# GpSimd makes h, TensorE takes its maximum over partitions, and integers are made further ahead

## The chip, the cores and the metric

The kernel runs on one core of one Trainium2 chip. A core has five engines that work beside each other, each through its own queue in order: TensorE (PE; its weight loads are shown apart as PEld), VectorE (DVE), ScalarE (ACT), GpSimd (POOL) and SyncE (SP), which issues most of the transfers between the chip's memory and the core's. The metric is the time of one execution on the device, in microseconds (us). Beside the times there is one profiled execution, with a record of every instruction; its times are counted from the start of its span.

## The reference

Two layers are computed on x, 2 x 2048 rows of 512 columns. First comes a cross attention to a context of 2 x 128 rows, then a feed-forward block whose values are rounded to integers at each step:

```
def act_qdq(x):                       # 16 bits, one scale for the whole tensor
    scale = max(max(abs(x)) / 32767, 1e-12)
    return clip(round(x / scale), -32768, 32767) * scale
x = x + softmax(layernorm(x) @ Wq @ key.T / sqrt(512)) @ value     # key, value = ctx @ Wkv
h = act_qdq(layernorm(x))                                          # (4096, 512)
up   = act_qdq(h @ lpbq_dequant(w_up).T)                           # (4096, 1536)
gate = act_qdq(h @ lpbq_dequant(w_gate).T)
gate = act_qdq(gate * fixed_qdq_u16(sigmoid(gate)))                # called p below
o    = act_qdq(gate * up)
x = x + o @ lpbq_dequant(w_down).T
```

`lpbq_dequant` rounds the weights to 4 bits with a scale for each block of 32. What shapes the kernel is that each `act_qdq` needs the largest absolute value of a whole tensor before the first of its values can be rounded.

## The kernel before, in words

The 4096 rows are worked on in 8 groups of 512 (NG = 8, TG = 512), each as 4 tiles of 128 rows (NJ = 4). The 512 columns are 4 chunks of 128 (ND = 4), the 1536 columns of the feed-forward block 12 chunks (NF), taken in three tiles of four (NK = 3, NQ = 4). Products of integers with weights are exact: an integer is split into parts (a high part `a` = n/4096, a low part n - 4096a, and a third), and so is a weight; the first two parts go into a sum q, the third into a sum e, and the result is q times a constant less e. One projected chunk is 8 matmuls for q and 4 for e (L528 and L532), each of 512 columns.

The code is a straight list of instructions. A scheduler gives each engine its order: an earlier line goes first if it is ready by the scheduler's own estimate. `in_order(a, b, ...)` (L158) fixes that b is issued behind a on their engine. Tiles come from pools, and a pool's tile waits until the tile that had its place has been read for the last time.

*Attention* (L257 to L506), in the order of a loop over i from 0 to 8 (L477). In step i the kernel loads x of group i + 2 (`load_x`, into a place of four `far` tiles, so it waits for the last reader of group i - 2), transposes the softmax of group i - 1 (`turn`, eT: four transposes on TensorE and a copy out of PSUM by ScalarE, L419), makes the scores of group i (`scores`), adds the attention of group i - 1 to x (`attend`: a matmul po, and on VectorE L432, which leaves the row's sum), starts group i + 1 (`front`: transposes, bn_stats), turns h of group i - 2 (`lift`: 16 transposes, two copies into hT by ScalarE, L472), and makes h of group i - 1 (`normalise`). `normalise` is a chain of small steps: the negative mean (VectorE, L446), four squares with a sum (ScalarE, L449), variance (L456), its inverse root as a power on GpSimd (L284), the product with the mean (L458), and four times h = x * rstd + nmean (ScalarE, L460). VectorE then takes the largest absolute value of h into hmax (L503). In step 8 the last group goes through this tile by tile (L490 to L494). Between these, `advance(gate_steps, n)` splits the gate's weights, a block in some ten steps, most of them on VectorE (L179 to L201).

*Gate* (L534 to L588). `over_partitions` (L136) reduces hmax to one value a partition (L140) and takes the maximum over partitions on GpSimd (L142). `act_scale` makes s_h and its inverse r_h (L151, L153). Four instructions on VectorE round group 0 chunk by chunk into hi[0] (L542), and `split_integers` (L229) makes its parts: for each chunk a (VectorE, L235), the cast to part 0 (ScalarE, L236), part 1 and part 2 (VectorE, L237, L238). Behind that, one activation loads the table of the sigmoid (L546), and the integers of groups 1 to 7 are made in one go, odd groups by VectorE (L549), even ones by ScalarE (L551). Then hT's place is given up, and two g4 tiles, a second home for parts and the place in which up's and down's weights are split take it. For each group and tile, four chunks are projected, evacuated by ScalarE (L579), lessened by e on VectorE with a running maximum (L580), and stored. After each chunk, `advance(steps, 1)` goes on with the weights.

*Up* (L597 to L791) goes through the 24 tiles from the last group to the first (`order`), each in two halves c = 2j and 2j + 1. For a half, TensorE makes two chunks, ScalarE evacuates them (L726), VectorE subtracts (L727), SP stores. `next_gelu` makes the rounded gate and its sigmoid for the next tile by three passes of ScalarE (L624 to L626) into one of three buffers; it is called in the first half of every tile and once more at c = 1 and c = 13. `integers_of_p` (L658) makes p from them on VectorE (L661) and stores it, at the head of each tile. `bound` (L667) takes the largest product of |up| and p in each half, which later tells from which half tile the largest o comes: `fetch_best` (L674) finds the row by partition and gathers it with two indirect transfers on GpSimd's queue (L685), of which the first waits for the stores of up. `load_down` (L694) loads down's weights into the places of up's weights that are done with. At the end, the largest |up| goes over partitions through TensorE (L764 to L769): m_u is transposed as 128 equal columns, and VectorE reduces the rows.

*Down* (L794 to L1024). From the three candidate maxima comes `top` on GpSimd (L791), from it a_o, and `scale_of_o` (L907) makes six small values: k_o, with which p * up is rounded, and s_o, q_o and e_o, with which sums are scaled on their way out. A flag tells whether the shortcut holds; its value is read by every engine for a branch (L926), which isn't taken here. Then 32 blocks of 128 rows are rounded (`round_o`), split and multiplied (L874, L882).

Of the kernel before, what the change touches and what calls it, by code (L numbers as in the profile page):

```python
# [49 lines left out]
F32 = mybir.dt.float32  # L50
# [13 lines left out]
P = 128  # L64
# [12 lines left out]
def tile_xattn_ffn(  # L77
# [58 lines left out]
    def over_partitions(*stats, name):  # L136
# [6 lines left out]
        return [a[:, i : i + 1] for i in range(len(stats))]  # L143

# [112 lines left out]
    with ExitStack() as c0:  # L257

        with ExitStack() as c1:
# [153 lines left out]
            def turn(g, e):  # L413
# [5 lines left out]
                nc.scalar.copy(eT, pe)  # L419
# [22 lines left out]
            def normalise(g, js, h, total, nmean, squares, ve, rstd):  # L442
# [16 lines left out]
                for j in js:  # L459
                    nc.scalar.activation(  # L460
                        h[:, j, :], xt[:, j, :], AF.Identity, bias=nmean[:, j : j + 1], scale=rstd[:, j : j + 1]
                    )
# [43 lines left out]
            lift(NG - 1, hs.pop(NG - 1))  # L506

# [15 lines left out]
        def project(w, parts, q, e):  # L523


            for c in range(ND):
                for s in range(2):
                    nc.tensor.matmul(  # L528
                        q, lhsT=w[:, s, c, :], rhs=parts[:, s, c, :], start=(c + s == 0), stop=(c + s == ND)
                    )  # L530
            for c in range(ND):
                nc.tensor.matmul(e, lhsT=w[:, 2, c, :], rhs=parts[:, 2, c, :], start=(c == 0), stop=(c == ND - 1))  # L532

        with ExitStack() as c2:  # L534
            wg = [load_parts(wg_d, f, "wg") for f in range(NF)]
            s_h, r_h = act_scale(*over_partitions(hmax, name="h"), "h")
# [4 lines left out]
            for c in range(ND):  # L541
                nc.vector.tensor_scalar(hi[0][:, c], hT[:, c, :TG], r_h, QMAX, ALU.mult, ALU.min)  # L542
            first = split_integers(wk1, homes[0], hi[0], [ND, TG], "g0", ND)

            table = const.tile([P, 1], F32, name="table")
            nc.scalar.activation(table, unit, AF.Sigmoid)  # L546
            for t in range(1, NG):
                if t % 2:
                    nc.vector.tensor_scalar(hi[t], hT[:, :, ts(t, TG)], r_h, QMAX, ALU.mult, ALU.min)  # L549
                else:  # L550
                    nc.scalar.activation(hi[t], hT[:, :, ts(t, TG)], AF.Copy, scale=r_h)  # L551
            hpool.__exit__(None, None, None)
            home1 = tc.tile_pool(name="parts1", bufs=1, side="right")
            homes.append(ctx.enter_context(home1))
            wk2 = c2.enter_context(tc.tile_pool(name="wkb2", bufs=2))
            wpp = c2.enter_context(tc.tile_pool(name="wprep", bufs=1))
# [3 lines left out]
            steps = chain(split_rows(wpp, ps_t, w_up, wu_d, "u"), split_down(wpp, ps_t))  # L560
            groups, wu = {}, []
            for t in range(NG):
# [8 lines left out]
                for k in range(NK):  # L571
                    n = t * NK + k
                    g4 = wk2.tile([P, NQ, TG], F32, tag="g4", name=f"g4_{n}")
# [474 lines left out]
```

## Time and profile before

| | us |
|---|---|
| runs shown: median of 3, lowest, highest | 1007.1, 1004.01, 1007.13 |
| the profiled execution: its own time | 1005.54 |
| its span | 1003.7 |
| attention, up to the last copy into hT | 0 to 173.0 |
| gate and up on TensorE | 177.0 to 720.0 |
| down, from the first matmul of o | 734.5 to 1000.7 |

The busy shares of the span are: PE 94%, PEld 76%, DVE 81%, ACT 55%, POOL 9%. A line of the page or of a table of stretches gives for each engine its busy time and the number of instructions; the last three numbers of a stretch are the granted TensorE clock (1.00 is full speed), the share of the DMA engines' time, and GB/s. A line of the timeline gives start, length, engine, line of the code, operation, output <- inputs, shape, count, and in square brackets how long the engine was idle before and what released it. Matmuls are pipelined, so a matmul's length is longer than its share: 24 of 512 columns at full clock take 5.44 us, 0.227 each.

### The profile page before, as it was taken

The numbers are of one execution on the slowest core, as the hardware profiler recorded it, in microseconds if no ns is written. First come the engines' busy times: TensorE is split into PE (matmuls) and PEld (weight loads), VectorE is DVE, ScalarE is ACT, GpSimd is POOL, SyncE is SP. The second block draws the span as 40 slices with busy tenths as digits, with TensorE's granted clock in tenths as the row PEclk, the third lists the DMA queues.
The fourth block names the chain that finished last, engine by engine and source line by source line (L and its number), as shares of the span: only waits on it lengthen the run. The fifth ranks groups of instructions, "written<-read, shape, count | busy, mean of one in ns | idle before, by whom it ended". The sixth has DMA issues, their size and how long they took to land. (4 is left out here: it accounts for less than half of the span.)

```text
span 1003.7 us, 11683 instructions
## 1 busy us (share of the span) xinstructions
PE 942.7 (94%) x4321; PEld 762.9 (76%) x4321; DVE 810.7 (81%) x1000; ACT 548.3 (55%) x652; POOL 89.6 (9%) x67
## 2 busy tenths in 40 slices
PE   6997884999999999999999999999779999999998
PEld 5765652788888878887788788888557888888886
DVE  4579874999998989645899789887889999888882
ACT  2277786532333223226998998897454445444331
POOL 0101111000000000000000000000011232222221
PEclk9999896999999999999999999999879999999999
DMA  9177652987886666698899798988885676755611
GB/s 345 32 304 283 220 220 79 401 313 303 330 355 248 265 210 210 224 353 328 306 363 375 258 366 328 378 320 328 288 311 215 206 269 222 250 190 160 245 66 43
DMA packets 103596, 263.72 MB, mean 263 GB/s; under 512 B 6064, under 2 KB 46000, under 8 KB 94832
## 3 DMA queue, kind: packets, MB, share of 16 engines
q1 hardware_dynamic: 102496, 259.02, 69.4%
q0 software_dynamic: 512, 2.88, 0.8%
q10 hardware_dynamic: 528, 1.05, 0.3%
q8 instruction: 34, 0.56, 0.2%
q14 instruction: 26, 0.21, 0.1%
HBM read 136.05 MB, written 126.88 MB: 262 GB/s over the span
## 5 line engine op out<-in xcount | busy, mean ns | idle before, releaser
L528 PE MATMUL q_g<-parts_g,wg 128*128 128x512 f32 x768 | 195.0, 394 | 5.1 <-ACT parts_g L236 5.1
L528 PEld LDWEIGHTS q_g<-parts_g,wg 128*128 128x128 f32 x768 | 143.5, 189 | 35.4 <-ACT parts_g L236 5.8
L579 ACT ACTIVATE g<-q_g 128x512 f32<-128x512 f32 x96 | 57.3, 599 | 169.6 <-PE q_g L528 158.9
L528 PE MATMUL q_u<-parts_u,wu 128*128 128x512 f32 x576 | 142.4, 390 | 0.6 <-ACT u L726 0.6
L528 PEld LDWEIGHTS q_u<-parts_u,wu 128*128 128x128 f32 x576 | 108.1, 188 | 23.3 <-ACT u L726 1.0
L874 PE MATMUL yq<-wd,o_parts 128*128 128x512 f32 x512 | 122.1, 391 | 0.0
L874 PEld LDWEIGHTS yq<-wd,o_parts 128*128 128x128 f32 x512 | 96.9, 189 | 20.3
L532 PE MATMUL e_g<-parts_g,wg 128*128 128x512 f32 x384 | 104.0, 392 | 0.1
L580 DVE CUSTOM_DVE_ANT_0 g<-g,e_g 128x512 f32<-128x512 f32 x96 | 64.4, 681 | 37.2 <-PE e_g L532 37.0
L532 PEld LDWEIGHTS e_g<-parts_g,wg 128*128 128x128 f32 x384 | 72.3, 189 | 15.6 <-DVE parts_g L238 0.5
L889 POOL TENSOR_TENSOR qx<-yqs,x 128x512 f32<-128x512 f32 x32 | 63.7, 1991 | 204.3 <-ACT yqs L887 167.9
L874 PE MATMUL yq<-first_wd,o_parts 128*128 128x512 f32 x256 | 65.5, 399 | 13.2 <-ACT o_parts L863 13.2
L887 ACT ACTIVATE yqs<-yq,q_o 128x512 f32<-128x512 f32 x32 | 22.0, 686 | 101.8 <-PE yq L874 101.8
L532 PE MATMUL e_u<-parts_u,wu 128*128 128x512 f32 x288 | 77.1, 390 | 0.0
L866 DVE SCALAR_TENSOR_TENSOR o_parts<-sa,oi 128x1536 fp32r<-128x1536 int16 (+2 forms) x41 | 62.8, 1548 | 15.6 <-PE ye L882 15.6
L863 ACT CAST o_parts<-sa 128x1536 fp32r<-128x1536 int16 (+2 forms) x41 | 48.6, 1189 | 43.9 <-DVE sa L860 43.9
L670 DVE CUSTOM_DVE_ANT_0 ua<-ua,pi 128x1024 f32<-128x1024 f32 x46 | 55.9, 1220 | 16.9 <-ACT ua L669 16.7
L862 DVE SCALAR_TENSOR_TENSOR o_parts<-sa,oi 128x1536 fp32r<-128x1536 int16 (+2 forms) x41 | 59.5, 1451 | 10.9 <-PE yq L874 8.5
L874 PEld LDWEIGHTS yq<-first_wd,o_parts 128*128 128x128 f32 x256 | 48.9, 192 | 24.4 <-ACT o_parts L863 14.2
L727 DVE TENSOR_TENSOR u<-u,e_u 128x1024 f32<-128x1024 f32 x47 | 56.9, 1216 | 12.0 <-ACT u L726 11.9
L661 DVE SCALAR_TENSOR_TENSOR pi<-gi,k_p,sq 128x2048 int16<-128x2048 int16 x24 | 56.4, 2349 | 9.7 <-ACT sq L626 9.7
L882 PE MATMUL ye<-wd,o_parts 128*128 128x512 f32 x256 | 63.2, 389 | 0.0
(185 smaller groups left out, 1553.7 us busy)
## 6 DMA issues: line engine op xcount, KB each, us to landing
gate_d<-g SPq DMA_DIRECT2D x24, 1024.0 KB, 5.5
up_d<-u SPq DMA_DIRECT2D x48, 512.0 KB, 7.2
gt<-gate_d SPq DMA_DIRECT2D x22, 1024.0 KB, 8.6
u<-up_d SPq DMA_DIRECT2D x21, 1024.0 KB, 6.5
parts_d<-parts_g SPq DMA_DIRECT2D x6, 3072.0 KB, 10.9
parts_u<-parts_d SPq DMA_DIRECT2D x6, 3072.0 KB, 13.4
p_d<-pi SPq DMA_DIRECT2D x24, 512.0 KB, 9.7
p<-p_d SPq DMA_DIRECT2D x84, 128.0 KB, 3.3
```

The lines of the kernel that those rows point to most:

```text
L528: nc.tensor.matmul(q, lhsT=w[:, s, c, :], rhs=parts[:, s, c, :], start=(c + s == 0), stop=(c + s == ND))
L532: nc.tensor.matmul(e, lhsT=w[:, 2, c, :], rhs=parts[:, 2, c, :], start=(c == 0), stop=(c == ND - 1))
L579: nc.scalar.activation(g4[:, i, :], q, AF.Copy, scale=1.0 + 1.0 / BASE)
L580: nc.vector.tensor_tensor_reduce(g4[:, i, :], g4[:, i, :], e, 1.0, LOWEST, ALU.subtract, ALU.max, gtop[:, m : m + 1])
L661: nc.vector.scalar_tensor_tensor(pi, gi, k_p, sq, ALU.mult, ALU.mult)
L670: nc.vector.tensor_tensor_reduce(ua, ua, pi, 1.0, 0.0, ALU.mult, ALU.max, pumax[:, c : c + 1])
L727: less = nc.vector.tensor_tensor(u4[:, both, :], u4[:, both, :], e, ALU.subtract)
L862: made.append(nc.vector.scalar_tensor_tensor(parts[1][:, c], sa[:, c], -BASE, oi[:, c], ALU.mult, ALU.add))
L866: return nc.vector.scalar_tensor_tensor(parts[2][:, c], sa[:, c], BASE + 1.0, oi[:, c], ALU.mult, ALU.subtract)
L874: nc.tensor.matmul(q, lhsT=parts[s][:, f, :], rhs=wd[f][:, s, :], start=(f + s == 0), stop=(f + s == NF))
L882: nc.tensor.matmul(e, lhsT=parts[2][:, f, :], rhs=wd[f][:, 2, :], start=(f == 0), stop=(f == NF - 1))
L889: nc.gpsimd.tensor_tensor(qx, qs, x1[:, m % NU, :], ALU.add)
```

## The change

It has six parts.

1. `normalise` makes h (L460) of groups 0 to 6 on GpSimd instead of ScalarE; the last group stays on ScalarE.
2. The copy of eT (L419) of the last group goes to VectorE.
3. The maximum of hmax over partitions goes through TensorE, as that of umax did; both now call one function. For h it is called at the end of the attention, behind the last `lift`.
4. `first_integers` makes the first group's parts by chunks, three of the four roundings by ScalarE, with all third parts behind the others. In the first tile TensorE makes the first two chunks' q ahead of their e. The integers of groups 1 to 7 are made one by one behind the subtractions and evacuations of the first tile; hT is given up after it, and `steps` begin with the second tile, two a chunk there.
5. In up, `next_gelu` is called once more at c = 1, 13, 19 and 31 (before: 1 and 13). `next_p` takes the place of `integers_of_p`: once in the first half of each tile, behind its evacuation, and once more at c = 17 and 27. One group of loads of down's weights goes ahead of the store of its half tile instead of behind it.
6. Of `scale_of_o`, only k_o is made ahead of the branch; the rest comes behind the first block's sums.

```diff
+    def over_partitions_by_pe(pool, tag, shape, stats, name):
+        m = const.tile([P, 1], F32, name=f"m_{name}")
+        nc.vector.tensor_reduce(m, stats, AX.X, ALU.max)
+        rows = pool.tile(shape, F32, tag=tag, name=f"rows_{name}")
+        rows = rows[:, 0, :P] if len(shape) == 3 else rows[:, :P]
+        nc.tensor.transpose(rows, m.to_broadcast([P, P]), ident)
+        a = const.tile([P, 1], F32, name=f"a_{name}")
+        nc.vector.tensor_reduce(a, rows, AX.X, ALU.max)
+        return a
...
-                nc.scalar.copy(eT, pe)
+                if g < NG - 1:
+                    nc.scalar.copy(eT, pe)
+                else:
+                    nc.vector.tensor_copy(eT, pe)
...
                 for j in js:
-                    nc.scalar.activation(
-                        h[:, j, :], xt[:, j, :], AF.Identity, bias=nmean[:, j : j + 1], scale=rstd[:, j : j + 1]
-                    )
+                    if g < NG - 1:
+                        nc.gpsimd.tensor_scalar(
+                            h[:, j, :], xt[:, j, :], rstd[:, j : j + 1], nmean[:, j : j + 1], ALU.mult, ALU.add
+                        )
+                    else:
+                        nc.scalar.activation(
...
             lift(NG - 1, hs.pop(NG - 1))
+            a_h = over_partitions_by_pe(ps_o, "o", [P, D], hmax, "h")
...
+        def first_integers(pool_a, r_h):
+            n = hi[0]
...
+            for c in range(ND):
+                if c == 0:
+                    made.append(nc.vector.tensor_scalar(n[:, c], hT[:, c, :TG], r_h, QMAX, ALU.mult, ALU.min))
+                else:
+                    rounded.append(nc.scalar.activation(n[:, c], hT[:, c, :TG], AF.Copy, scale=r_h))
+                made.append(nc.vector.tensor_scalar(a[:, c], n[:, c], 1.0 / BASE, None, ALU.mult))
+                casts.append(nc.scalar.copy(parts[:, 0, c], a[:, c]))
+                made.append(
+                    nc.vector.scalar_tensor_tensor(parts[:, 1, c], a[:, c], -BASE, n[:, c], ALU.mult, ALU.add)
+                )
+                if c:
+                    in_order(rounded[c - 1], casts[c - 1])
+            for c in range(ND):
+                made.append(
+                    nc.vector.scalar_tensor_tensor(
+                        parts[:, 2, c], a[:, c], BASE + 1.0, n[:, c], ALU.mult, ALU.subtract
+                    )
+                )
+            in_order(*made)
+            return parts, casts[-1]
...
-            for t in range(1, NG):
-                if t % 2:
-                    nc.vector.tensor_scalar(hi[t], hT[:, :, ts(t, TG)], r_h, QMAX, ALU.mult, ALU.min)
-                else:
-                    nc.scalar.activation(hi[t], hT[:, :, ts(t, TG)], AF.Copy, scale=r_h)
-            hpool.__exit__(None, None, None)
...
+                    if n == 0:
+                        for i in range(2):
+                            project_q(wg[i], parts, sums[i][0])
...
+                        if n == 0:
+                            in_order(subtracted, integers_of_h(2 * i + 1))
+                            if i < NQ - 1:
+                                in_order(evacuated, integers_of_h(2 * i + 2))
+                        if n:
+                            advance(steps, 2 if n == 1 else 1)
...
+        more_gelu = (1, NH // 4 + 1, 3 * NH // 8 + 1, 5 * NH // 8 + 1)
+        more_p = (NH // 3 + 1, NH // 2 + 3)
...
-            if j:
-                pi = integers_of_p(j)
...
+                if t == 0 and k == 0 and h == 1:
+                    load_down(range(NE, NE + NQ), slice(0, 2))
                 stored = nc.sync.dma_start(out=up_d[c], in_=u4[:, both, :])
-                if h == 0:
+                if h == 0 or c in more_gelu:
                     next_gelu()
-                if c == 0:
-                    pi = integers_of_p(0)
-
-                if c in (1, NH // 4 + 1):
-                    next_gelu()
+                if h == 0 or c in more_p:
+                    next_p()
+                pi = kept_p[j % NK]
...
-            if t == 0 and k == 0:
-                load_down(range(NE, NE + NQ), slice(0, 2))
...
-        def scale_of_o(a_o):
+        def factor_of_o():
             nc.vector.tensor_scalar(k_o, a_o, 1.0 / QMAX, tiny_o, ALU.mult, ALU.max)
             nc.vector.reciprocal(k_o, k_o)
+
+        def scale_of_o():
             nc.vector.tensor_tensor(s_o, a_o, s_pu, ALU.mult)
...
-        scale_of_o(a_o)
+        factor_of_o()
...
                 if m == 0:
+                    scale_of_o()
                     in_order(casts[-1], *round_up(ui, 0, P, P))
```

## The prediction

> **What bounds the kernel now.** I read the page first, then the table of stretches, the waits of each engine, and the timeline of the three places where TensorE stands still. The first line of the page says that TensorE is the bound over most of the span:
>
> ```profile
> PE 942.7 (94%) x4321; PEld 762.9 (76%) x4321; DVE 810.7 (81%) x1000; ACT 548.3 (55%) x652; POOL 89.6 (9%) x67
> ```
>
> From 190 us to 720 us, and from 745 us to the end, the projections run back to back: in the stretches of 20 us from 500 to 560 TensorE is busy 20.00 of 20.00. An edit gains there only what little TensorE waits: by its waits in the up stage 1.4 us for ScalarE's evacuation (L726), 0.9 for VectorE's maximum (L580) and 0.3 for VectorE's subtraction. So the change can win in the attention, whose end looks like this in the table of stretches (stretch, length, then busy us of each engine, granted clock, DMA):
>
> ```profile
> 114.00:130.00 16.00, 14.21 (x83) 9.87 (x84) 13.37 (x29) 11.96 (x27) 3.46 (x2) 1.00 0.41 158
> 130.00:141.00 11.00, 8.30 (x56) 6.16 (x55) 8.90 (x22) 9.73 (x20) 3.44 (x2) 1.00 0.73 279
> 141.00:152.00 11.00, 8.03 (x43) 4.82 (x41) 6.52 (x15) 10.14 (x25) 1.03 (x2) 1.00 0.30 127
> 152.00:163.00 11.00, 8.50 (x24) 4.25 (x24) 5.85 (x16) 7.08 (x14) 1.01 (x1) 0.69 0.01 1
> 163.00:177.00 14.00, 3.28 (x16) 2.41 (x16) 6.80 (x23) 10.23 (x16) 2.55 (x5) 0.62 0.45 177
> ```
>
> The reader sees two regimes. Up to about 130 us VectorE is the busiest of the small engines (13.37 of 16), because it also splits the gate's weights. From 130 to 152 us it is ScalarE (10.14 of 11), and from 152 us nobody: this is a chain of single waits, and the granted clock falls to 0.62. The timeline names the links (start, length, engine, line, operation, idle before and releaser):
>
> ```profile
> 153.17 0.57 ACT L419 COPY eT<-pe 128x512 f32<-128x512 f32 x1
> 153.79 5.49 PE L431 MATMUL po<-vsb,eT 128*128 128x512 f32 x6 [4.77 <-ACT eT L419]
> 157.88 2.29 DVE L169 TENSOR_REDUCE hmax<-h 128x1 f32<-128x2048 f32 x1 [1.21 <-ACT h L460]
> 160.08 0.74 DVE L432 SCALAR_TENSOR_TENSOR xt<-po,den,xt 128x512 f32<-128x512 f32 x1
> 174.00 0.15 DVE L151 TENSOR_SCALAR s_h<-a_h 128x1 f32<-128x1 f32 x1 [4.04 <-POOL a_h L142]
> 177.02 2.10 PE L528 MATMUL q_g<-parts_g,wg 128*128 128x512 f32 x4 [5.06 <-ACT parts_g L236]
> ```
>
> The last group's eT waits on ScalarE behind h of group 5 and four squares of group 6; its second attend waits on VectorE behind hmax of group 6, which waits for ScalarE's h; the maximum over partitions costs 4.04 us; the first gate matmul comes 2.67 us after r_h (174.35).
>
> **The change, part by part.** Times are those of before's profiled execution: 1005.54 us, of which the span is 1003.7 and 1.84 lie around it. The median of the runs shown is 1007.1 (1004.01 to 1007.13), 1.6 above; the sum is made against 1005.54.
>
> (1) *h of groups 0 to 6 on GpSimd, 128x512, 28 of them.* ScalarE loses 28 x 0.804 us = 22.5 (row L460). GpSimd gains 28 of an operation that before doesn't show. Nearest rows on GpSimd: affine select 128x128 0.29, memset 128x1 0.10, so 0.10 + 4 x 0.19 = 0.86 for 512 columns; from above, the two-input add 128x512 (L889) 1.28 undisturbed; from below ScalarE's own 0.73 from one start to the next. I take 0.95, nearest to the select: 3.8 us a group against 2.93. What it meets is VectorE:
>
> ```profile
> 114.14 1.75 DVE L187 TENSOR_TENSOR w_g<-wi_g,ws_g 128x1536 f32<-128x1536 int16 x1
> 114.30 2.45 POOL L284 TENSOR_TENSOR row<-row,mhalf 128x4 f32<-128x4 f32 x1 [16.62 <-DVE nmx L323]
> 751.66 1.32 POOL L889 TENSOR_TENSOR qx<-yqs,x 128x512 f32<-128x512 f32 x1 [4.51 <-ACT yqs L887]
> 751.94 1.59 DVE L862 SCALAR_TENSOR_TENSOR o_parts<-sa,oi 128x512 fp32r<-128x512 int16 x1
> ```
>
> GpSimd's power takes 1.01 alone and 2.45 when it starts inside L187: it ends 0.86 after L187 does. The other way round, L862 of 512 columns takes 0.69 alone and 1.59 when GpSimd's add was first: 0.90 lost. In the attention from 45 us on VectorE has 14 such operations (L185, L187, L198, L201, 1.75 each), 24.5 us in all, the last at 130 us, and four of 0.96 (L196).
>
> The Trainium skill, "SBUF — State Buffer", section "Who interferes with whom", says that a VectorE instruction with two SBUF inputs and a GpSimd instruction that reads SBUF shut each other out for a whole instruction, and that tensor_reduce is never part of it. The two pairs of rows above agree (0.86 and 0.90). By that rule hmax, bn_stats and the attends out of PSUM go on undisturbed. It speaks against this edit up to 130 us, and is worked out as a rival below.
>
> Up to 130 us: GpSimd works 3.8 of some 17 us a step, so perhaps 4 of the 14 operations are met, at half an operation: 2 us lost on VectorE. Against it stand VectorE's waits for ScalarE (45 to 180 us: hmax for h 5.6, L196 for wsp_g 5.6, L456 for h 3.1), part of which goes since ScalarE is 11.72 us freer by 130 us. I take 0; bounds 14 x 0.95 = 13 lost, 6 gained. xt is released later by up to 1 us, and so are the loads of x: that of the last group (issued 120.00) is first read by bn_stats at 125.17, with nothing to spare, but last at 138.76, so other VectorE work can go ahead; without that cover it costs the 1 us.
>
> (2) *The end of the attention: h of groups 5 and 6 off ScalarE, eT of the last group on VectorE.* Without h(5) the last two exponentials (147.68 to 148.55) follow at 144.6, so pe is there by about 147. VectorE copies it either right behind the attends of group 6 (147.4), or behind hmax(5), which now waits until 144.85 + 3.8 = 148.65 and ends at 150.95; a copy out of PSUM of 512 columns took it 0.68 (L380). eT is ready at 148.1 or 151.65 in place of 153.74. Squares of group 6 start at 147.7, behind L446, in place of 150.34, its power ends about 151.9, GpSimd's h at 155.9 (157.85 before), hmax(6) at 158.2 (160.17). If the attends stay behind hmax(6), 2.0 us are won; if all four go ahead of it, 153.8 + 3.6 = 157.4 in place of 162.8, 5.4. I take 3.5. The last group's own chain (square, power, normalise on ScalarE, hmax, 162.8 to 169.97) stays; its powers queue behind h(6) on GpSimd, free at 155.9, before the first of them is due.
>
> (3) *Maximum over partitions through TensorE.* The same for u, in before, takes 0.99 us from m_u (721.50) to the first reader of a_u (722.49). For h: m_h at 169.80, s_h at 174.00, 4.2 us. Were the transpose at once on TensorE, 3.2 would go. But TensorE then works on the eight last transposes (169.99 to 171.96), ahead in the program: 171.96 + 0.66 = 172.62, 1.4 won. I take 1.6 (bounds 0 and 3.2); late next is ScalarE's last hT copy (172.00 to 173.01), which holds its first rounding.
>
> (4) *First group by chunks.* First matmul: rounding 0.48, sa 0.29, cast 0.57 on its way, ScalarE meanwhile at the second chunk: r_h + 1.45 in place of 2.67. VectorE needs 0.48 + 4 x (0.25 + 0.60) = 3.9 for the first two parts, and 2.4 more for the third, in place of 7.3 us; TensorE does both q (16 matmuls) meanwhile, the first eight cold at 0.43 (3.4 us), so the two e can start at r_h + 6.7 and the four blocks end at about r_h + 6.7 + 1.8 + 5.4 = 13.9; before they ended at 190.26, r_h + 15.9. Won 1.9 (a remaining wait makes it 0.5, a warm clock 3). The other groups' integers go behind each block: ScalarE 0.6 + 2.0, VectorE 0.7 + 1.2 a block, under TensorE's 2.72, so they are hidden; uncovered, 0.4 as at 187.24. hT, the split of up's weights and SP's load of w_u come 3 us later; two steps a block in the second tile make up for it.
>
> (5) *Integers further ahead in up.* Two more sets of three ScalarE passes (2.0 + 2.0 + 1.9) come early, at half tiles 19 and 31, and the last two sets and two p (2.35 each) are gone from the end. ScalarE was full after the first such extra (19.97 of 20 from 480 to 500, TensorE 1.22 idle) and not after the second (520 to 540: 19.79, TensorE 0 idle). So 0 to 1.2 each; I take 0.5 lost in all. At the end:
>
> ```profile
> 720.47 1.08 POOL L685 DMA_INDIRECT best<-up_d,row x1 [261.86 <-DMA up_d<-u]
> 729.62 1.23 DVE L786 CUSTOM_DVE_ANT_0 product_b<-ui_b,best 128x1024 f32<-128x1024 int16 x1 [3.12 <-DMA best<-p_d,row]
> 734.52 3.06 PEld L874 LDWEIGHTS yq<-first_wd,o_parts 128*128 128x128 f32 x8 [12.59 <-ACT o_parts L863]
> ```
>
> TensorE's 12.6 us wait hangs on the gather, that on the landing of the store of half tile 45, that on its subtraction at 710.71, which queued 1.6 us behind umax and a bound on VectorE (its sums were there at 709.08). With the p gone (701.62) this queue clears: 1.4. The four loads of wd (2 MB, 705.55) go in front of that store on SP by one tile half, about 2 us sooner, and clear the queues sooner: up to 1.5 more. I take 2.0 won (0 to 3.5); late next would be the product of the resident tiles (726.41).
>
> (6) *Scale of o split.* Four small operations leave the chain ahead of the branch; they stretch it from 732.10 to 732.40. 0.2 won (0 to 0.3); they come back in m = 0 under TensorE's sums.
>
> Sum: 0 - 3.5 - 1.6 - 1.9 + 0.5 - 2.0 - 0.2 = -8.7; 1005.5 - 8.7 = **996.8 us**.
>
> **Rivals.**
> - *ScalarE's relief also shortens the steps before 130 us* (bound of part 1): 6 more, 990.8. For it: 14 us of VectorE's waits end at ScalarE. Against: VectorE is busy 83% from 45 to 130 us. Chance 0.20.
> - *Given back in up*: both further extras stall TensorE by 1.22 each, and the store of half tile 45 is held by its landing, not by VectorE: +1.9 and +2.0, 1000.7. Chance 0.15.
> - *Little of it happens*: the attends stay behind hmax, hmax waits longer for GpSimd's h than for ScalarE's, and parts 2 and 5 go to 0 while 3, 4 and 6 hold 3.7 less up's 2.4: about 1004. Chance 0.10.
> - *Slower: GpSimd shuts VectorE out.* Place: the steps with weight splitting, 45 to 130 us, where VectorE paces. Price 0.95 for each operation met. From 10 of the 14 on (10 x 0.95 = 9.5 against 8.7) the change loses; all 14 give 996.8 + 13.3 = 1010. For it: each power or add that met VectorE paid in full; GpSimd's four h come in a row, just as VectorE is at the weights. Against: GpSimd is at work in a fifth of a step. Chance 0.10.
> The forecast has 0.45.
>
> **The numbers.** 0.3% (3 us) is what a measurement of this kernel can tell from no change. Faster by more: 0.45 + 0.20 + 0.15 = 0.80; the 1004 case is within it, 0.10; slower 0.10. From 989 to 1004: left out are the slower case, half of the 1004 case and a little below 989.
>
> **What would show it.** Part 1: rows of GpSimd of 128x512 at 0.9 to 1.0, and VectorE's 1.75 us rows near 2.7 where they were met. Part 2: eT of the last group on VectorE by 151.7, no ScalarE wait of po. Part 3: s_h 1 to 3 us after m_h. Part 4: first L528 1.5 us behind r_h. Part 5: the first gather 2 us sooner after TensorE's half tile 45, and the stretches from 540 to 640 still full on TensorE. Wrong if GpSimd's h takes 2 us or more, or if the first gate matmul isn't 5 us or more sooner than 177.0.

## The result and the profile after

| | us |
|---|---|
| before, 20 runs: median, lowest, highest | 1006.67, 1004.01, 1010.04 |
| after, 20 runs on the same chip | 1000.9, 996.66, 1005.03 |
| ratio after / before, with its 95% interval | 0.9952 [0.994, 0.9963] |
| the same two kernels once more, 6 and 11 runs | 1000.16, 1006.6: 0.9928 [0.9908, 0.9949] |
| after, the profiled execution and its span | 1005.03, 1003.2 |

The change makes the kernel faster by 5 to 7 us (the medians differ by 5.8 and 6.4 us, the ratios make it 4.8 and 7.2). The forecast was 996.8 us, 8.7 less than the profiled execution of before. The sign and the range (989 to 1004) hold; a fifth to nearly a half of the gain is missing. The profiled execution of after is the slowest of its 20, so times within it are compared here by stages, and a second profile of each kernel stands beside the first.

In the page, ScalarE and VectorE have less to do and GpSimd more, as intended; TensorE is as full as before:

```profile
PE 941.6 (94%) x4322; PEld 763.4 (76%) x4322; DVE 805.6 (80%) x999; ACT 529.0 (53%) x626; POOL 110.6 (11%) x94
```

The table of stretches of the attention (stretch, length, busy us of PE, PEld, DVE, ACT, POOL, granted clock, DMA):

```profile
114.00:130.00 16.00, 14.76 (x74) 10.09 (x74) 11.97 (x24) 8.01 (x20) 5.99 (x6) 0.81 0.54 207
130.00:141.00 11.00, 8.01 (x49) 5.72 (x48) 8.28 (x17) 5.19 (x12) 5.30 (x5) 0.98 0.57 215
141.00:152.00 11.00, 10.36 (x50) 7.03 (x49) 5.63 (x21) 6.47 (x18) 5.04 (x6) 0.87 0.32 137
152.00:163.00 11.00, 7.11 (x29) 3.47 (x30) 6.92 (x20) 8.24 (x19) 4.28 (x6) 1.00 0.36 150
163.00:177.00 14.00, 8.62 (x32) 6.21 (x32) 12.51 (x30) 11.47 (x17) 1.82 (x4) 0.67 0.46 181
```

From 130 to 152 us ScalarE is busy 11.7 us in place of 19.9: the relief is there. But the end of the attention comes no sooner: the reduction of hmax over its columns (m_h), the last step ahead of the maximum over partitions, begins at 168.92 us in place of 169.80, and in the second profiles at 169.24 in place of 168.01. The timeline of the joints shows the same (start, length, engine, line, operation, idle before and releaser):

```profile
154.22 0.68 DVE L433 COPY eT<-pe 128x512 f32<-128x512 f32 x1
162.79 2.29 DVE L180 TENSOR_REDUCE hmax<-h 128x1 f32<-128x2048 f32 x1 [2.52 <-POOL h L475]
169.98 0.15 DVE L162 TENSOR_SCALAR s_h<-a_h 128x1 f32<-128x1 f32 x1
172.26 1.22 PE L552 MATMUL q_g<-parts_g,wg 128*128 128x512 f32 x2 [2.64 <-ACT parts_g L572]
715.34 1.19 POOL L761 DMA_INDIRECT best<-up_d,row  x1 [253.95 <-DVE row L756]
730.72 3.06 PEld L945 LDWEIGHTS yq<-first_wd,o_parts 128*128 128x128 f32 x8 [9.12 <-ACT o_parts L934]
```

eT of the last group is made by VectorE now, and still a microsecond later than before (153.17); hmax of group 6 waits 2.5 us for GpSimd's h. Behind that the joints are shorter: s_h follows 1.06 us after m_h (4.20 before), the first transfer of the gather begins 4.3 us ahead of up's end (0.5 behind it before), and TensorE's weight loads wait 9.1 us for down in place of 12.6.

Where a lead over before arises and where it goes (us from the span's start, first and second profile):

| | before | after | lead |
|---|---|---|---|
| reduction of hmax begins (m_h) | 169.8, 168.0 | 168.9, 169.2 | -1.2 to 0.9 |
| first gate matmul begins | 177.0, 175.4 | 172.3, 172.6 | 3 to 5 |
| gate ends | 454.7, 453.8 | 452.6, 453.3 | 0.5 to 2 |
| up ends | 719.95, 721.3 | 719.6, 719.5 | 0.3 to 2 |
| first matmul of down begins | 734.5, 735.8 | 730.7, 730.6 | 4 to 5 |
| its 144th ends | 770.4, 771.9 | 770.9, 768.0 | -0.5 to 4 |

The lead at the first gate matmul therefore arises wholly behind m_h, in parts 3 and 4; parts 1 and 2 together gave the attention nothing that these profiles show.

### The profile page after: what moved, and what is told of

It reads as the page before. It is cut to its first block, busy times and chain, and to the rows that moved or that the text cites. A ratio compares the mean times of both kernels' runs of the same rounds, so it can differ in the third digit from the quotient of the medians.

```text
span 1003.2 us, 11704 instructions
## 1 busy us (share of the span) xinstructions
PE 941.6 (94%) x4322; PEld 763.4 (76%) x4322; DVE 805.6 (80%) x999; ACT 529.0 (53%) x626; POOL 110.6 (11%) x94
## 5 line engine op out<-in xcount | busy, mean ns | idle before, releaser
L937 DVE SCALAR_TENSOR_TENSOR o_parts<-sa,oi 128x1536 fp32r<-128x1536 int16 (+2 forms) x41 | 59.7, 1474 | 20.5 <-PE ye L953 20.5
L933 DVE SCALAR_TENSOR_TENSOR o_parts<-sa,oi 128x1536 fp32r<-128x1536 int16 (+2 forms) x41 | 59.5, 1451 | 13.2 <-PE yq L945 11.4
L558 PEld LDWEIGHTS e_u<-parts_u,wu 128*128 128x128 f32 x288 | 54.0, 188 | 11.9 <-DVE u L805 0.7
```

Of the source, the lines that this page charges most:

```text
L933: made.append(nc.vector.scalar_tensor_tensor(parts[1][:, c], sa[:, c], -BASE, oi[:, c], ALU.mult, ALU.add))
L937: return nc.vector.scalar_tensor_tensor(parts[2][:, c], sa[:, c], BASE + 1.0, oi[:, c], ALU.mult, ALU.subtract)
```

## The experiments

Fourteen runs were made: the two kernels again, and twelve others. All but before_again, a single execution for its profile, were timed against before on the same chip. m_h is from one profile each; kernels with the same order of instructions in the attention differ in it by up to 2.3 us (h_act and act_upold).

| run | what it is | ratio, 95% interval | m_h us |
|---|---|---|---|
| after_again | after | 0.9928 [0.9908, 0.9949] | 169.2 |
| before_again | before | | 168.0 |
| h_act | after without part 1 | 0.9886 [0.9868, 0.9904] | 165.2 |
| ordered | after, order of two queues fixed | 0.989 [0.9873, 0.9907] | 162.4 |
| h_only | before with part 1 | 1.0065 [1.0049, 1.008] | 176.8 |
| eT_only | before with part 2 | 0.9939 [0.9928, 0.9951] | 162.8 |
| up_old | after without part 5 | 0.9933 [0.991, 0.9956] | 170.7 |
| act_upold | after without parts 1 and 5 | 0.9897 [0.9873, 0.9921] | 162.9 |
| eT_act | without parts 1, 2 and 5 | 0.9942 [0.9926, 0.9959] | 169.6 |
| first_old | without parts 1, 4 and 5 | 0.9877 [0.9859, 0.9894] | 164.9 |
| eT_p | eT_only, last p product later | 0.9934 [0.9923, 0.9946] | 163.0 |
| loads_ahead | eT_only, down's loads earlier | 0.9945 [0.9924, 0.9966] | 164.4 |
| best | ordered, without part 5, loads of up's tiles first | 0.9866 [0.9848, 0.9884] | 162.8 |
| warm | best, with matmuls in TensorE's waits | 0.9832 [0.9817, 0.9846] | 162.8 |

### The same two kernels again

> The changed kernel once more, for a second profile. Its one profiled execution so far took 1005.03 us, 4.1 above its median of 1000.9, and lost 3.6 us in one wait at the start of down: the matmuls of the fourth block stood until 764.4 us, because the loads of up's tiles of the second group were issued at 746.8 us and landed 11.2 us later. Theory A (the leads of 4.8 us at the first gate matmul and of 3.8 us at the first matmul of down are real, and are used up by new waits behind them: VectorE late in the first 150 us of the gate, and the loads of up's tiles late at the start of down): the ratio is again 0.994 to 0.997, and the second profile has the same two leads and the same two places where they shrink, even if its total is nearer to 1001. Theory B (that profile was unusual, and a typical execution keeps the leads): the wait at the fourth block is under 1.5 us, and the end comes 3 us or more earlier than in before's profile.

> The kernel before once more, for a second profile. Theory A: TensorE's wait at the start of down is again 12 us or so, the waits within the first 150 us of the gate are again under 1 us together, and the fourth block of down waits less than 1 us; the first gate matmul comes at 177 us to within 0.5. Theory B: these figures move by 2 us or more from one profile of the same kernel to the next, so that single profiles can't be set against each other.

The second profile of after took 1002.13 us, with the joints of the table above, the same two stalls of TensorE, which end at 258 and 291 us (1.4 and 1.2; 1.5 and 1.2 in the first), and 2.4 us of wait at the fourth block of down (3.6 in the first). Before again has no such stall in that part of the gate and under 0.5 us at the fourth block, and its first matmul of down again comes 14.6 us behind the end of up; its m_h and first gate matmul come 1.8 and 1.6 us sooner than in its first profile, more than A allowed. So the leads at the first matmul of the gate and of down are real, and shrink at the same two places (A). Two things don't fit A: the ratio, 0.9928, lies below its range, and the end comes over 3 us sooner than in before, as B had asked.

### Part 1: h on GpSimd

```diff
 # h_act: all groups take the branch of the last one
-                    if g < NG - 1:
+                    if False:
                         nc.gpsimd.tensor_scalar(
...
```

> The changed kernel with h of all eight groups on ScalarE, as in the kernel before; all other parts stay. Theory A (GpSimd's h is worth little: its own operation is as quick as ScalarE's, VectorE waits for it about as much as it waited for ScalarE, and what is won behind it is used up in the gate and down): the first gate matmul is 0.5 to 1.5 us later, the end 0 to 1 us later: ratio 0.995 to 0.996. Rival 1 (GpSimd shuts VectorE out in the attention, and that is where the forecast's gain went): without it the first gate matmul comes 2 us or more sooner, ratio 0.992 to 0.993. Rival 2 (relief of ScalarE is most of the gain): the first gate matmul comes 3 us later, ratio 0.997 to 0.999.

Without part 1 the changed kernel takes 995.87 us, 4.3 less than with it (1000.16), and the first gate matmul comes at 168.4 us, 4 sooner. Theory A fell: part 1 is no near-nothing, it is the missing gain. That is rival 1's result, and more than it asked for (0.9886 against 0.992 to 0.993), but its mechanism isn't there. In the trace of after, GpSimd's h (duration ns: least, median, most):

```profile
L475 POOL TENSOR_SCALAR h<-xt,row,row x28: 767/773/2334, 61.8 to 162.0; 128x512 f32<-128x512 f32 x28
```

So 0.77 us for one, and 3.02 for four in a row, about as quick as ScalarE's 2.93; two of the seven fours took longer, 4.59 and 4.30. Of the rows of VectorE with two SBUF inputs between 40 and 168 us none is longer than in before (at most 1.76 us in both). What differs is who waits. The waits of VectorE in the attention (engine, line, releaser: us, times, longest), first after, then h_act:

```profile
DVE hmax L180 <- POOL h L475: 15.4, 7, 3.2
```

```profile
DVE hmax L180 <- ACT h L479: 5.5, 5, 3.0
```

And a place where after falls behind, first the two rows of before, then the timeline of after:

```profile
135.80 0.75 DVE L432 SCALAR_TENSOR_TENSOR xt<-po,den,xt 128x512 f32<-128x512 f32 x1
136.47 2.28 DVE L169 TENSOR_REDUCE hmax<-h 128x1 f32<-128x2048 f32 x1
```

```profile
131.91 4.30 POOL L475 TENSOR_SCALAR h<-xt,row,row 128x512 f32<-128x512 f32 x4 [0.46 <-DVE row L472]
133.31 0.74 DVE L446 SCALAR_TENSOR_TENSOR xt<-po,den,xt 128x512 f32<-128x512 f32 x1
136.25 2.29 DVE L180 TENSOR_REDUCE hmax<-h 128x1 f32<-128x2048 f32 x1 [2.19 <-POOL h L475]
138.53 0.72 DVE L446 SCALAR_TENSOR_TENSOR xt<-po,den,xt 128x512 f32<-128x512 f32 x1
139.18 0.74 DVE L446 SCALAR_TENSOR_TENSOR xt<-po,den,xt 128x512 f32<-128x512 f32 x1
140.52 0.73 DVE L446 SCALAR_TENSOR_TENSOR xt<-po,den,xt 128x512 f32<-128x512 f32 x1
```

The scheduler now puts hmax of group 4 behind one of group 5's four additions and ahead of the other three; in before and h_act it stands behind all four. That its estimate of the new engine's time makes the difference is likely, but not shown. VectorE stands 2.2 us for GpSimd, and group 5's sums are complete at 141.2 in place of 136.5 in before and 136.0 in h_act. GpSimd's own time has a share in this wait: its four h took 4.30 us here in place of 3.02, and the first of them began inside a VectorE row with two SBUF inputs (131.56 to 133.31). In the whole attention, the copies hT on ScalarE wait longer for their transposes (18.1 us, 5.0 in h_act). Theory C was formed on this: it is the order. The test leaves h on GpSimd and only fixes where its readers stand:

```diff
 # ordered: hmax and the transposes of h behind the next group's attention
+                    in_order(added, abs_max(hmax[:, i - 2 : i - 1], hs[i - 2], AX.XY))
-                    lift(i - 2, hs.pop(i - 2))
+                    lift(i - 2, hs.pop(i - 2), summed)   # each transpose: in_order(summed, it)
...
-                    abs_max(hmax[:, i - 1 : i], hs[i - 1], AX.XY)
```

> The changed kernel, h of groups 0 to 6 still on GpSimd, with the order of two queues fixed: the largest value of a group's h (VectorE) and the transposes of its h (TensorE) stand behind the next group's attention, where the kernel with h on ScalarE has them for the later groups. Theory C (GpSimd's h costs 4.5 us by order alone: readers of h stand ahead of other ready work on VectorE and TensorE, 15.4 us of waits of VectorE for GpSimd's h, though GpSimd is as quick as ScalarE and no VectorE row is longer): the first gate matmul comes at 168.5 to 170.0 us in place of 172.3 to 172.6, ratio 0.988 to 0.991. Rival 1 (GpSimd's h is itself late, by its own length and by VectorE's locks, whatever the order): first gate matmul at 172 or later, ratio 0.993 to 0.996.

994.56 us, and the first gate matmul at 165.8, sooner than theory C had asked for. GpSimd's rows are as in after (769/773/2334 ns, again two of them long), the wait is not:

```profile
DVE hmax L180 <- POOL h L476: 2.6, 1, 2.6
```

So the cost of part 1 was the order of its readers. With that order fixed, part 1 neither costs nor wins: 0.989 against 0.9886 without it. Not run is the fixed order with h on ScalarE, so a gain of the fix for itself is not ruled out; h_act has that order for the later groups as it is. Whether the cost stood alone or only beside the other parts:

> The kernel before with part 1 alone: h of groups 0 to 6 on GpSimd, with no other edit. The order that the scheduler then makes on VectorE is that of the changed kernel: the largest value of a group's h stands ahead of three or four of the next group's additions. If part 1 costs by itself what undoing it won in the changed kernel (4.5 us): the reduction of hmax comes at 171 to 174 us in place of 169.8, ratio 1.002 to 1.0045. Rival (the prediction's step: no cost, and with the softmax copy still on ScalarE the relief of ScalarE shows as a gain of 2 to 4 us at the end of the attention): ratio 0.996 to 0.998.

It costs 6.3 us by itself, more than expected (1012.26 against 1005.92; ratio 1.0065, where 1.002 to 1.0045 was expected). The waits of hmax are those of after, and the softmax copy, still on ScalarE and 4.6 us later than in before, is late as well. First its waits, then its timeline:

```profile
DVE hmax L169 <- POOL h L461: 16.5, 7, 3.7
157.77 0.57 ACT L419 COPY eT<-pe 128x512 f32<-128x512 f32 x1
```

### Part 2: the last copy of eT on VectorE

```diff
 # eT_only: before with this alone; eT_act: act_upold without it
-                nc.scalar.copy(eT, pe)
+                if g < NG - 1:
+                    nc.scalar.copy(eT, pe)
+                else:
+                    nc.vector.tensor_copy(eT, pe)
```

> As the run with parts 1 and 5 undone, and part 2 undone as well (the copy of the last group's softmax on ScalarE again). If part 2 is what brought the end of the attention forward by 4.4 us in the run with h on ScalarE (reduction of hmax at 165.2 against 169.8 us): the reduction comes at 169.0 to 170.0 and the ratio is 4 us worse than that of the run it is built on. Rival (the order of the last groups' small steps changed for another reason, and the copy is worth 0 to 1.5): the reduction comes before 167.

> The kernel before with part 2 alone: the copy of the last group's softmax goes to VectorE. In the run with parts 1 and 5 undone this copy was worth 4.5 us (0.9897 with it, 0.9942 without). If it holds by itself: the reduction of hmax comes at 165 to 166 us in place of 169.8, ratio 0.995 to 0.9965. Rival (the gain needs the other parts, or is swallowed behind the attention): ratio 0.998 to 1.0.

Undone, it costs 5.2 us (999.56 against 994.33, m_h back at 169.6). Alone, it takes 6.0 us off before, more than expected: a single copy is worth as much as the whole change. In the timeline of eT_only:

```profile
148.08 0.66 DVE L422 COPY eT<-pe 128x512 f32<-128x512 f32 x1
148.79 3.96 PE L434 MATMUL po<-vsb,eT 128*128 128x512 f32 x8 [1.78 <-DVE eT L422]
153.05 0.74 DVE L435 SCALAR_TENSOR_TENSOR xt<-po,den,xt 128x512 f32<-128x512 f32 x1
156.06 3.47 DVE L169 TENSOR_REDUCE hmax<-h 128x1 f32<-128x2048 f32 x3 [1.23 <-ACT h L463]
```

The copy comes 5.1 us sooner than in before, and all four additions of the last group now stand ahead of hmax of group 6, so the last one ends at 153.8 in place of 162.8.

### Part 5: passes and products further ahead in up

```diff
 # up_old: the calls of up where before has them
-                if t == 0 and k == 0 and h == 1:
-                    load_down(range(NE, NE + NQ), slice(0, 2))
-                if h == 0 or c in more_gelu: ...        # four extra calls
-                if h == 0 or c in more_p: ...           # next_p, two extra calls
...
+            ... next_p() at a tile's head; next_gelu() also at c = 1 and 13; load_down behind the tile
 # act_upold: up_old and h_act together
```

> The changed kernel with its fifth part undone: in up, the gate's rounding three passes and p's products are issued where the kernel before has them, and down's weights are loaded behind the tile's store. All that comes ahead of up stays as changed. Theory A (part 5's gain at the end of up is swallowed by the loads of up's tiles at the start of down): first matmul of down 2 us later than with part 5, end of the kernel within 1 us of it: ratio 0.995 to 0.997 against 0.995 with it. Rival (part 5's extra passes are what costs: new stalls in up of 1.2 us each): without it the kernel is 1 to 2.5 us faster, ratio 0.9925 to 0.994. The prediction's own step would make it 1.5 us slower: 0.9965.

> The changed kernel with its first part undone (h of all groups on ScalarE) and its fifth part undone (up's extra passes and products back where they were). If the two costs add: 4.5 us for part 1, and for part 5 the 2.3 to 5 us that up was longer in the profiles with part 5 less what it gives at the end of up, so ratio 0.984 to 0.988. Rival (part 5 costs nothing in the sum, as the timed runs of the kernel without it say: 0.9933 against 0.9928): ratio 0.9875 to 0.9895, as with h on ScalarE alone (0.9886).

Undoing part 5 changes nothing that these runs can tell, with part 1 (0.9933 and 0.9928) and without (0.9897 and 0.9886). The profiles show two sides. Two profiles of after have stalls of TensorE at 680 and 688 us (0.9 to 1.7 and 0.3 us), which up_old lacks. Up as a whole takes 265.3 and 266.1 us there and 262.7 in up_old; but profiles without the extra passes go from 262.6 to 267.3 (before and before_again 264.3 and 266.6), so this doesn't show a cost. And the first matmul of down comes 11.5 us behind the end of up in up_old too, though the calls are back where before has them (14.6 there). The scheduler had not made before's order again: the four loads of down's weights went out 19.9 us ahead of up's end, in before 14.4. So up_old doesn't undo the earlier loads, and what shortens that wait was asked apart:

```diff
 # eT_p: the last product of p behind the subtraction of half tile 45
+            if j == LAST:
+                in_order(less, made)
 # loads_ahead: the four loads of down's weights ahead of the store of their half tile
+                if t == 0 and k == 0 and h == 1:
+                    load_down(range(NE, NE + NQ), slice(0, 2))
...
-            if t == 0 and k == 0:
-                load_down(range(NE, NE + NQ), slice(0, 2))
```

> As the run with part 2 alone on the kernel before, and the last p product of VectorE fixed behind the subtraction of half tile 45; nothing else of part 5. In the kernel before it stands ahead of the subtraction of half tile 43 and waits for ScalarE. If the step of the prediction is right that this queue holds the gather: the gather's first transfer starts 4 us ahead of the end of up in place of 0.5 behind it, and the first matmul of down comes 11.1 to 11.5 us behind the end of up in place of 14.6; of these 3 us the start of down keeps 1 to 3, ratio 0.001 to 0.003 below that of part 2 alone. Rival (it was the earlier loads of down's weights or the two extra products): still 14 us or more.

> As the run with part 2 alone, and of part 5 only its last clause: the group of four loads of down's weights (2 MB) goes ahead of the store of its half tile on SyncE; the products of p stay where the kernel before has them. If the place of these loads is what holds the last stores of up and p, and with them the gather: the loads are issued 19 us or more ahead of the end of up in place of 14.4, the gather starts 3 us or more sooner, first matmul of down 11.1 to 12.5 us behind the end of up in place of 14.1 to 14.6; ratio 0.001 to 0.003 below that of part 2 alone (0.9939). Rival (the place of the loads and of the last product must both change): still 13.5 us or more.

Moving the product doesn't shorten the wait (14.7 us; 14.1 in eT_only): the gather is released by the landing of a store of p, 0.5 us ahead of up's end. Moving the loads does: they go out at 695.15, 22 us ahead of up's end, and the gather starts 3 us ahead of that end:

```profile
695.15 2.23 SPq L702 DMA_DIRECT2D wd<-wd_d  x4
714.18 1.07 POOL L688 DMA_INDIRECT best<-up_d,row  x1 [261.33 <-ACT u L739]
728.51 3.73 PE L877 MATMUL yq<-first_wd,o_parts 128*128 128x512 f32 x8 [9.19 <-ACT o_parts L866]
```

The first matmul of down comes 11.4 us behind up's end. Yet the total doesn't move (0.9945 against 0.9939): from there to the 144th matmul it takes 39.7 us, 36.1 in eT_only. What stands there is SyncE's queue, with the same rows in loads_ahead and in after; here those of after:

```profile
739.78 6.87 SPq L892 DMA_DIRECT2D p<-p_d  x10
746.76 1.56 SPq L882 DMA_DIRECT2D u<-up_d  x3
754.21 1.15 ACT L908 ACTIVATE ui<-u,r_u 128x1024 int16<-128x1024 f32 x1 [2.76 <-DMA u<-up_d]
760.84 3.06 PE L945 MATMUL yq<-first_wd,o_parts 128*128 128x512 f32 x8 [3.57 <-ACT o_parts L934]
```

Ten loads of p, needed from the fifth block on, are issued ahead of the loads of up's tiles. ScalarE's next roundings (ui) wait for these, and the cast for the fourth block stands behind them in its queue.

### Part 4: the first group by chunks

```diff
 # first_old: act_upold with before's gate start
-            first, last_cast = first_integers(wk1, r_h)
+            for c in range(ND): ...                     # four roundings on VectorE
+            first = split_integers(wk1, homes[0], hi[0], [ND, TG], "g0", ND)
+            for t in range(1, NG):
+                integers_of_h(t)                        # all at once; steps begin with the first tile
```

> As the run with parts 1 and 5 undone, and part 4 undone as well (first group's parts and all integers as in the kernel before). The prediction's step 4 said that part 4 wins 1.9 us: this run would be 1.9 slower than the one it is built on. Theory A (part 4 wins 0.7 at the first gate matmul and nothing in the first four blocks, and by starting the split of up's weights a tile later it makes the two stalls of 1.4 us at 257 and 290 us): this run is 0 to 3 us faster, without those two stalls, and its first 720 gate matmuls take 174.7 to 176 us in place of 177.5.

994.28 us against 994.33: no difference. In the profiles part 4 wins and loses. The first gate matmul comes at r_h + 1.94 us (2.67 before), but 48 matmuls are done in after at r_h + 15.8 (15.9 in before): the first 16 of them take 6.6 us with the granted clock at 0.5, where the working had eight cold ones. In act_upold, where the clock rose sooner, they are done at r_h + 14.7 (15.9 in first_old). And the two stalls of 1.2 to 1.6 us at 250 to 291 us, of which the first waits for VectorE, are in after, h_act, ordered and act_upold, and not in first_old, whose first 720 gate matmuls take 174.6 us in place of 177.3; it gives 1.9 us back later (one wait of 1.9 ahead of a weight transpose at 368 us; before has one of 1.8 at 376).

### A version put together

```diff
 # best: ordered, up as in up_old, and on SyncE:
+                    if t == NS:
+                        in_order(loaded[-1], one)       # p of the second group behind up's tiles
 # warm: best, and matmuls that nobody reads
+            keep_warm(...)                              # 9, 12, 8 and 12 transposes in four waits
+        for i in range(34):
+            nc.tensor.matmul(warm[:, i % 2, :], lhsT=first_wd[:, 0, 0, :P], rhs=first_wd[:, 0, 1, :], ...)
```

> A version put together from what the runs showed: h of groups 0 to 6 on GpSimd with the order fixed (first gate matmul at 165.8), up as before part 5 (up 2 to 3 us shorter in the profiles), and on SyncE the loads of up's tiles of the second group of down ahead of the loads of p, so that the wait at the fourth block of down (1.9 us with the cold start behind it) goes. If the costs add: ratio 0.983 to 0.986. Rival (the wait at the fourth block moves to p's loads, and part 5 counts for nothing): 0.987 to 0.990, as with the order alone.

> As the version put together, with matmuls whose results nobody reads in TensorE's waits: 41 transposes of 128 columns in the four waits at the end of the attention, and 34 matmuls of 512 columns between the end of up and the first matmul of down. In the profiles so far the granted clock falls to 0.5 some 4.8 us after TensorE goes idle and stays there 3.9 us into the work of down (36 matmuls take 10.3 us in place of 8.2) and 5 us into the gate (24 take 8.2 in place of 5.4). If busy matmuls keep the clock: 2 us at the start of down, and 1 to 3 us at the gate, ratio 0.003 to 0.005 below the version put together. Rival (they delay what is due behind them, or the clock falls all the same): no gain, or up to 2 us lost.

best takes 992.52 us, at the edge between the two expectations. The wait at the fourth block, 1.7 us in ordered, is gone, and the fifth waits 0.4 (first matmul of down to the end of the 144th: 35.9 us, in ordered 36.8). warm takes 989.09 us, 3.4 less than best, 17 less than before. The stretches of best, then of warm; the number behind the five engines is the granted clock:

```profile
152.00:163.00 11.00, 6.68 (x32) 5.11 (x33) 6.71 (x18) 7.37 (x11) 5.01 (x8) 0.63 0.23 96
163.00:177.00 14.00, 11.36 (x39) 8.87 (x38) 10.01 (x25) 11.78 (x15) 0.00 (x0) 0.68 0.90 364
```

```profile
152.00:163.00 11.00, 7.41 (x57) 5.90 (x56) 6.68 (x18) 7.47 (x12) 4.99 (x8) 1.00 0.23 96
163.00:177.00 14.00, 12.34 (x59) 9.98 (x59) 12.71 (x29) 13.63 (x17) 0.00 (x0) 1.00 0.94 376
```

With the clock kept, the first 24 gate matmuls take 5.9 us in place of 8.4, and the first 36 of down 10.0 in place of 11.4: together 3.9 us, about the gain.

## Why the prediction was right in sign and wrong in size

The sign of being wrong that the prediction named came true: the first gate matmul is 4.7 and 4.4 us sooner than 177.0, not 5.

- **Step 1 failed: "I take 0".** Measured: 4.3 us lost inside the change (h_act), 6.3 alone (h_only). The bounds (13 lost, 6 gained) held it, but for another reason than the one given. The working asked what GpSimd's instruction costs and whom it shuts out: it took 0.77 us a piece (0.95 estimated), and no VectorE row was longer. It didn't ask what a new engine does to the order in the queues of those that read h. The ordered run shows that the loss goes when only this order is changed. The rival "GpSimd shuts VectorE out" had the right sign for the part and the wrong mechanism. The rival "Little of it happens" (chance 0.10) was nearest in mechanism: hmax waited 15.4 us for GpSimd's h, where in before it waited 5.6 for ScalarE's, and m_h came no sooner. But at about 1004 us it was too slow: part 3 gave more, and the 2.4 us that it charged for up didn't show in the sum.
- **Step 2, -3.5: the copy was worth more, 6.0 by itself and 4.5 to 5.2 beside the others.** The working put the gain down to h of groups 5 and 6 leaving ScalarE as well. eT_only shows that h needn't leave it. In after the gain was mostly eaten: h of group 5 ended at 152.0 us, where the working had 148.65, so the copy, behind hmax of group 5 on VectorE, came at 154.22. That GpSimd would be free before the last group's powers were due was wrong: they began at 162.71, when h of group 6 ended there.
- **Step 3, -1.6: right mechanism, larger.** m_h to s_h went from 4.20 to 1.06 us, 3.1 won, at the upper bound: the transpose of m_h ran at once (169.14 us), since the last transposes of h had been issued by then. No run undoes part 3 by itself.
- **Step 4, -1.9: 0** (first_old). The early start is won (0.7 of the expected 1.2). At the 48th matmul 0.1 us was left of it in after, and 1.2 us were won in act_upold, as the clock went; the two stalls of the gate take that back. That these come from the later start on up's weights, which the step had called covered, fits their being gone in first_old, but first_old undoes the rest of part 4 as well.
- **Step 5, +0.5 and -2.0: 0 in sum** (up_old and act_upold for the passes and products, loads_ahead for the loads). The wait ahead of down shrank by 3.5 us, at its upper bound, by the loads (loads_ahead) and not by the cleared queue of VectorE (eT_p); what the extra passes cost up is not clear of the spread between profiles; the start of down then gave up 1 to 4, on the loads of up's tiles, which no step had looked at.
- **Step 6, -0.2: as said.** From a_o to the first o it is 1.61 us in place of 1.86.

Without part 1, steps 2 to 6 were forecast at -8.7 us and gave -10.7 (995.87 against 1006.6). That this sum was near is in part luck: steps 2 and 3 were put too low by 2.5 to 4 us together, steps 4 and 5 too high by 3.4. The term at zero was off by 4.3 us, and nothing made up for it.

On what GpSimd paid, the Trainium skill, "SBUF — State Buffer", section "Who interferes with whom", says that a VectorE instruction with two SBUF inputs contends with a GpSimd instruction that reads SBUF, over ports that are locked for one of them. In after two of GpSimd's 28 rows took 2.33 and 2.05 us, both begun inside a VectorE row of 1.75, and no VectorE row grew: the rule shows here on one side, and cost 2.8 us of GpSimd's time in all.

## What to carry to other kernels

When work moves to another engine, list its readers on every queue and ask what ready work stands behind each of them: here the scheduler put them too early, and a fixed order got the loss back. Try the one copy or small step that the critical chain waits for alone before a bundle of parts. A joint that is made shorter hands its gain to the next queue that was on time until then (here the loads at the start of down), so look there in the same profile.

## What the runs showed of the hardware that was not expected

- The clock was worth 3.4 us (best to warm) for 75 matmuls whose results nobody reads, put into waits that are 1.2 to 8.9 us long in best. Only the softmax copy, part 2, was worth clearly more. The Trainium skill, "TensorE: Matmul & The Clock Gate", section "Part 1: The HAM clock gate (the 'warmup' mystery)", says that an idle window of about 3.4 us halves the clock and a busy one restores it. The rows agree: between the end of up and down, with 34 matmuls in the wait, the clock is low for one stretch of 3.4 us only (717.3 to 720.7), in best for 13.7 (714.6 to 728.2).
- GpSimd's multiply and add with a scalar for each partition (128x512) took 0.773 us, four in a row 3.02: about as quick as ScalarE's activation of that shape, 2.93 for four.
